# First diffusion step: where the rows of a block are scaled and split

## The chip, the cores and the metric

One core of a Trainium2 chip runs the whole kernel. The metric is the device time of one execution in microseconds (us). Five queues of instructions matter: TensorE (PE, matrix products and transposes), VectorE (DVE), ScalarE (ACT), GpSimd (POOL, which here also issues the stores) and SyncE (SP, which here issues the loads). Each of them works through its own instructions in order and waits for the others by semaphores.

## The reference

The program has two layers over 2708 nodes with 512 features. The first is graph attention with eight heads, and the change doesn't touch it. The second is a diffusion of two steps; its core, with `S` the adjacency matrix plus the unit matrix and `X` the cleared rows, is:

```python
Rf = S / S.sum(axis=1, keepdims=True)
Rb = S / S.sum(axis=0)[:, None]
Xf, Xb, Xa = X, X, X
for s in range(2):
    A = adj_from_feats(Xa, W1, W2, W3)   # logits, sorted, kept up to 0.9 of the softmax mass
    Xf = Rf @ Xf
    Xb = Rb @ Xb
    Xa = A @ Xa
    Z = Z + (Xf @ U1[s] + Xb @ U2[s] + Xa @ U3[s])
```

`A` keeps, in each row, the largest logits until their softmax reaches 0.9, and divides by their sum. In the first step `Xf` and `Xb` both start from `X`, so `S @ X` is computed once and its rows are scaled twice: by 1/row sum for `Xf` and by 1/column sum for `Xb`.

## The kernel before

The rows are cut into 22 tiles of 128 (the last has 20 rows), the tiles into 11 pairs, and two pairs make a group of four tiles (the last group has two). The second layer runs the loop `for g in range(-1, NP)` (line 1183), once for each of its two steps. One turn of the loop, called block g here, does these things for pair g and its neighbours:

- the logits of pair g + 2: `lg[g + 2].products()` (lines 511 to 524). TensorE multiplies (line 521), ScalarE copies the product from PSUM into the tile `p` (line 523). `p` has four buffers, two pairs of tiles, so these copies wait until the search of pair g has ended.
- the search for the cut of pair g + 1: `search` (line 584 on). VectorE goes over the row of logits in a few rounds (line 629), then, in `finish`, takes out the next values (lines 806 and 808) and writes the kept values into `keep` (line 730). A switch follows that is hardly ever taken (line 890) and a reciprocal (line 907). `finish` stands behind `late()`, so everything that `late` gives VectorE to do comes before it in VectorE's queue.
- the attention product of pair g: `attended` (line 1008 on), twelve steps, six for each of the two tiles. In each, TensorE transposes four 128 x 128 pieces of `keep` (line 1016), ScalarE copies them to `at` (line 1020) and TensorE multiplies them with the values (line 1035).
- the exponentials and looks of pair g + 2, which prepare its search: a list of 19 steps named `fills`, mostly ScalarE work of 2.55 us over a whole row (lines 553 and 560). The argument `first` of `attended` says from which step on they are dealt out: two at a step up to the ninth, then one, and one each at six places of `mixed`. `first` is 3, and 7 in block 0. What is left over follows at the end of the block.
- the three products with `U1`, `U2`, `U3`: `mixed` (line 1060 on), called the U phase here: twelve times a load of `u_k` and its matrix products (line 1076). Then come the keys of the next step (`project`, line 160) and the sum `yo` (lines 1089 to 1095).
- `S @ X`: `part` (line 943 on). Block g works on half of the 22 products of one group: odd blocks finish what even blocks begin. A product (line 967) is a load of 512 KB (`hl`) and one of 256 KB (`s_r`) and eight matrix products into four PSUM tiles, which are held until the group is complete. When the second half is done, each of the four tiles is scaled twice: `scaled` (line 970 on) copies it from PSUM with the factor (ScalarE, line 977, tile `xe`, four buffers), stores it to `xfb_d` (POOL, line 978) and splits it into a high and a low part by `split_rows` (VectorE, lines 181 and 182, tile `split_hl`, two buffers), which are stored to `fhl_d` or `bhl_d` (POOL, line 183). These two are read in the second step alone, `xfb_d` in the U phases of the group's own pairs, by `diffused` (line 1000).

The order on TensorE, ScalarE, VectorE and SyncE is that in which the program text issues the instructions; GpSimd's order is set by a scheduler. The text has a list `others` with the block's products and scalings, from which `paced` takes a few at each step:

```python
others = left + part(half, g + 2)
...
if not last:
    paced(others, 1 + i)
```

So in the first step (`last` is false) one is taken at each of the first six steps of `attended`, two at each of the last six, and one with each `u_k`. In an odd block the 11 products and the first scalings so fall into `attended` and the rest of the eight scalings into the U phase. The eight of block -1 are left over to block 0: four ahead of its logits and four after them.

Of the kernel before, what the change touches and what calls it, by code (L numbers as in the profile page):

```python
# [53 lines left out]
def kernel(  # L54
# [19 lines left out]
    nc = tc.nc  # L74
# [127 lines left out]
    with ExitStack() as l0:  # L202
# [13 lines left out]
        with tc.tile_pool(name="l0w", bufs=1) as wp, tc.tile_pool(name="l0p", bufs=2) as pp, \  # L216
# [44 lines left out]
            for t in range(NT):  # L261
                pr = rows[t]
# [651 lines left out]
    for s in range(STEPS):  # L914
        last = s == STEPS - 1
        with ExitStack() as st:
# [26 lines left out]
            def part(half, b):  # L943

                if b // 2 >= len(quads):
                    return []
                quad = quads[b // 2]  # L950
                first = b % 2 == 0
                w = len(quad) * P
                hl_d = (fhl_d if first else bhl_d) if last else vhl_d
                cs = range(NT) if last else range(0, NT // 2) if first else range(NT // 2, NT)
                steps = []

                def product(c):
                    if c == 0:
                        half[:] = [ps_s.tile([P, D], F32, name=f"q{i}") for i in range(len(quad))]
                    hl = sp.tile([P, 2, D], F32R, name="hl", bufs=3)  # L960
                    nc.sync.dma_start(out=hl.bitcast(F32), in_=hl_d[c * P:(c + 1) * P])
                    s_r = sp.tile([P, 2 * G * P], F32R, name="s_r")
                    nc.sync.dma_start(out=s_r[:, :w].bitcast(F32),
                                      in_=s_d[c * P:(c + 1) * P, quad[0] * P:quad[0] * P + w])
                    for j in range(len(quad)):
                        for h in range(2):
                            nc.tensor.matmul(half[j], lhsT=s_r[:, j * P:(j + 1) * P], rhs=hl[:, h],  # L967
                                             start=(c == 0 and h == 0), stop=(c == NT - 1 and h == 1))

                def scaled(t, ps, i, inv, to):  # L970
                    pr = rows[t]

                    if last and b < 2 and t % 2:
                        x = work.tile([P, D], F32, name="xw", bufs=2)
                    else:
                        x = work.tile([P, D], F32, name="xe", bufs=2 if last else 4)
                    nc.scalar.activation(x[:pr], ps[:pr], AF.Copy, scale=inv[:pr, t:t + 1])  # L977
                    nc.gpsimd.dma_start(out=xfb_d[i, cols[t], :], in_=x[:pr])
                    if not last:
                        split_rows(parts, nc.vector, x[:pr], t, to)  # L980

                steps += [lambda c=c: product(c) for c in cs]
                if last or not first:
                    for j, t in enumerate(quad):
                        if first or not last:
                            steps.append(lambda j=j, t=t: scaled(t, half[j], 0, rinv, fhl_d))
                        if not first:
                            steps.append(lambda j=j, t=t: scaled(t, half[j], 1, cinv, bhl_d))
                return steps

            def paced(steps, n):
                for step in steps[:n]:
# [12 lines left out]
            def attended(grp, keep, rden, fills, others, then, first=3):  # L1005

                def turned(i, t, cs):
                    pr = rows[t]
                    pt = ps_t.tile([P, TG, P], F32, name="t")
                    at = work.tile([P, TG, P], F32, name="at")
                    for j, c in enumerate(cs):
                        nc.tensor.transpose(pt[:rows[c], j, :pr], keep[i][:pr, cols[c]], ident[:pr, :pr])  # L1016
                    full = sum(rows[c] == P for c in cs)
                    for r, j0, j1 in ((P, 0, full), (rows[cs[-1]], full, len(cs))):
                        if j0 < j1:
                            nc.scalar.copy(at[:r, j0:j1, :pr], pt[:r, j0:j1, :pr])  # L1020
                    return at

                steps = [(i, t, cs) for i, t in enumerate(grp) for cs in tgroups]
                at = turned(*steps[0])
                xa = []
                total = len(others)
                for n, (i, t, cs) in enumerate(steps):
                    pr = rows[t]
                    nxt = turned(*steps[n + 1]) if n + 1 < len(steps) else then()
                    if n >= first:  # L1030
                        paced(fills, 1 + i if last else 1 if n > 8 else 2)
                    if cs[0] == 0:
                        pa = ps_a.tile([P, D], F32, name="a")
                    for j, c in enumerate(cs):
                        nc.tensor.matmul(pa[:pr], lhsT=at[:rows[c], j, :pr], rhs=va[:rows[c], c, :],  # L1035
                                         start=(c == 0), stop=(c == NT - 1))
                    if not last:
                        paced(others, 1 + i)
                    elif i or len(grp) == 1:
                        paced(others, (total + 10) // 13)  # L1040
                    if cs[-1] == NT - 1:
                        xa.append(work.tile([P, D], F32, name="xa"))
                        nc.scalar.activation(xa[i][:pr], pa[:pr], AF.Copy, scale=rden[:pr, i:i + 1])  # L1043
                        if not last:
                            nc.gpsimd.dma_start(out=xa_d[cols[t], :], in_=xa[i][:pr])
                    at = nxt
                    yield
                return xa, at
# [8 lines left out]
            def turned_rows(grp, v):  # L1057
                return [transposed(up, ps_t, v[i], rows[t], "v_t") for i, t in enumerate(grp)]

            def mixed(grp, v_t, xf, xb, xa, others, fills, final=False):  # L1060

# [6 lines left out]
                for n, u in enumerate((u3, u1, u2) if final else (u1, u2, u3)):  # L1070
                    nxt = turned_rows(grp, ((xf, xb) if final else (xb, xa))[n]) if n < 2 else None
                    for k in range(KD):
                        u_k = up.tile([P, D], F32, name="u_k", bufs=4 if last else 3)
                        nc.sync.dma_start(out=u_k, in_=u[s, k * P:(k + 1) * P, :])  # L1074
                        for i, t in enumerate(grp):
                            nc.tensor.matmul(pz[i][:rows[t]], lhsT=v_t[i][:, k, :rows[t]], rhs=u_k,  # L1076
                                             start=(n == 0 and k == 0), stop=(n == 2 and k == KD - 1))
                        paced(others, 1)
                        if n < 2 and k < 3:
                            paced(fills, 1)  # L1080
                    if n == 2 and not last and not final:
                        for i, t in enumerate(grp):
                            project(small, ps_t.tile([P, 512], F32, name="t"), v_t[i], t, s + 1)
                    v_t = nxt
                out_ = []
                for i, t in enumerate(grp):
                    pr = rows[t]
# [76 lines left out]
            with tc.manual_schedule(engines={PE, ACT, DVE, SP}):  # L1164
# [9 lines left out]
                half = []  # L1174
                lg += [Logits(pools, s, grp, keys, rank) for grp in pairs[1:2]]
                lg[1].queries()
                for step in part(half, 0):
                    step()
                values()
                done = []  # L1180
                ready = None
                looks, left = [], []
                for g in range(-1, NP):

                    fills = []

                    held = len(left)
                    paced(left, held if last else held // 2)
                    others = left + part(half, g + 2)
                    left = []  # L1190
                    if g == 0 and last:
                        paced(others, 4)
                    if g + 2 < NP:
                        lg[g + 2].products()
                    if g + 3 < NP:
# [4 lines left out]

                    rows_in = []
                    if g >= 0:
                        others.insert(0 if g else len(others) // 3, lambda g=g: rows_in.extend(diffused(pairs[g])))
                        final = g == NP - 1 and not last
                        att = attended(pairs[g], *ready, fills, others,
                                       lambda: None if final else turned_rows(pairs[g], rows_in[0]),
                                       3 if g else len(tgroups) + 1)
                    if g == 0:

                        paced(others, held - held // 2 if not last else 0)  # L1210
                        while looks:
                            next(att)
                            paced(looks, 2)

                    def early(g=g):
                        if g + 2 < NP:
# [3 lines left out]
                    def late(g=g):  # L1220
                        if g >= 0:
                            if g:
                                paced(others, 1)
                            xa, v_t = rest_of(att)
                            done.extend(mixed(pairs[g], v_t, *rows_in, xa, others, fills, final))
                            paced(others, len(others))
                            paced(fills, len(fills))
                            return
# [49 lines left out]
```

## Time and profile before

| | us |
|---|---|
| median of three runs | 3710.2 (3706.5 to 3715.3) |
| profiled execution | 3708.3 |
| span of its trace | 3706.5 |
| the first diffusion step in it, about | 1090 to 2300 |
| one block of it, from line 160 to line 160 | 102 to 110, in blocks 2 to 7 |

The profile has one execution. A line of a timeline names its start and length, the engine, the source line, the operation with its output and inputs, and in square brackets how long the engine had been idle before it and who ended the wait. A line of the waits names the waiting engine and instruction, the instruction that released it, the sum of such waits, their number and the longest. By stretches, from line 160 of one block to line 160 of the next, blocks 2 to 5 look like this (columns: stretch, its length, then the busy time and number of instructions of TensorE, its weight loads, VectorE, ScalarE and GpSimd, the granted clock of TensorE, the busy share of the DMA engines and what they moved):

```profile
1413.40:1520.40 107.00, 98.51 (x334) 55.59 (x333) 69.44 (x181) 60.61 (x74) 17.05 (x27) 0.95 0.41 136
1520.40:1623.70 103.30, 97.90 (x333) 54.66 (x332) 40.41 (x60) 64.22 (x82) 21.79 (x43) 0.98 0.58 201
1623.70:1730.00 106.30, 98.15 (x334) 55.16 (x333) 69.18 (x181) 60.61 (x74) 16.79 (x27) 0.97 0.41 137
1730.00:1831.90 101.90, 96.51 (x334) 53.96 (x333) 39.04 (x60) 64.22 (x82) 21.82 (x43) 1.00 0.57 204
```

All four have the same matrix products. The odd ones (second and fourth line) have the scalings besides: more ScalarE work, more stores, and less of VectorE's, because part of the search of an odd block lies beyond the cut.

### The profile page before, as it was taken

To read this page: it belongs to the slowest core of one execution; us is meant where nothing else is said; L and a number is where in the kernel's file an instruction comes from. 1 tells how busy PE (TensorE), PEld (TensorE's weight loads), DVE (VectorE), ACT (ScalarE), POOL (GpSimd) and SP (SyncE) were. 2 spreads that over 40 slices of the span, in tenths; PEclk is the share of its full clock that TensorE was granted. 3 is DMA by queue.
4 is the path that set the end of the run, shared out by engine and by line. 5 is a ranking of instruction groups with operands and counts; after the bars stand their busy time and mean duration, and the time that the engine had idled before them with its cause. 6 is when DMAs were issued, how large, how long until landed. Compare 5 with 4: busy or idle time off the path is not lost. (4 is left out here: it accounts for less than half of the span.)

```text
span 3706.5 us, 35338 instructions
## 1 busy us (share of the span) xinstructions
PE 3367.4 (91%) x11143; PEld 1754.4 (47%) x11143; DVE 2612.9 (70%) x4820; ACT 1541.5 (42%) x2334; POOL 799.6 (22%) x1119
## 2 busy tenths in 40 slices
PE   7998999998966988989899899688999999999898
PEld 4433333333444545545455453445655565556452
DVE  4588888889957637365463651969988779777991
ACT  2343212111114674655666612345654556445511
POOL 4114140514331112121202121302112111121101
PEclk9999999999978999999999999999999999999999
DMA  3477424233228445454535353966556665566552
GB/s 113 152 252 243 137 80 150 80 105 103 74 87 278 164 157 187 145 183 149 205 131 196 128 191 100 302 203 225 175 187 208 233 216 204 183 213 234 201 201 66
DMA packets 276459, 634.08 MB, mean 171 GB/s; under 512 B 37210, under 2 KB 70442, under 8 KB 273244
## 3 DMA queue, kind: packets, MB, share of 16 engines
q1 hardware_dynamic: 249183, 540.99, 44.2%
q0 software_dynamic: 27024, 90.30, 6.3%
q8 instruction: 89, 1.46, 0.2%
q14 instruction: 163, 1.33, 0.1%
HBM read 509.07 MB, written 122.10 MB: 170 GB/s over the span
## 5 line engine op out<-in xcount | busy, mean ns | idle before, releaser
L1035 PE MATMUL a<-va,at 128*128 128x512 f32 (+2 forms) x1936 | 890.1, 599 | 14.0 <-ACT at L1020 13.5
L967 PE MATMUL q<-hl,s_r 128*128 128x512 f32 x2904 | 820.9, 429 | 62.5 <-DMA s_r<-s_d 62.2
L429 PE MATMUL po<-e,fw 128*65 128x512 f32 (+4 forms) x2112 | 838.7, 552 | 34.3 <-DVE e L427 21.8
L427 DVE SCALAR_TENSOR_TENSOR e<-r_b,kk,a_c 128x512 f32<-128x512 f32 (+4 forms) x1056 | 751.8, 741 | 73.5 <-PE po L429 23.7
L967 PEld LDWEIGHTS q<-hl,s_r 128*128 128x128 f32 x2904 | 544.4, 190 | 307.5 <-issue 133.2
L553 ACT ACTIVATE junk_a<-p,nth 128x2708 uint8<-128x2708 f32 (+1 forms) x240 | 613.1, 2554 | 70.6 <-POOL nth L572 66.8
L429 PEld LDWEIGHTS po<-e,fw 128*65 128x65 f32 (+1 forms) x2112 | 286.2, 140 | 546.7 <-issue 269.2
L1035 PEld LDWEIGHTS a<-va,at 128*128 128x128 f32 (+2 forms) x1936 | 337.1, 187 | 379.4 <-issue 342.7
L1076 PE MATMUL a<-u_k,v_t 128*128 128x512 f32 (+1 forms) x1056 | 489.9, 601 | 22.3 <-ACT xa L1043 15.4
L629 DVE SCALAR_TENSOR_TENSOR junk<-p,th 128x2708 bf16<-128x2708 f32 (+1 forms) x132 | 401.2, 3039 | 4.0
L1020 ACT COPY at<-t 128x512 f32<-128x512 f32 (+3 forms) x308 | 140.4, 477 | 494.5 <-PE t L1016 494.1
L1076 PEld LDWEIGHTS a<-u_k,v_t 128*128 128x128 f32 (+1 forms) x1056 | 188.9, 187 | 242.1 <-issue 182.9
L521 PE MATMUL t<-keys,q_t 128*128 128x452 f32 x528 | 167.1, 443 | 118.4 <-ACT p L523 98.1
L181 DVE TENSOR_SCALAR split_hl<-xe 128x512 int32<-128x512 int32 (+1 forms) x44 | 19.1, 434 | 257.1 <-ACT xe L977 210.7
L808 DVE MAX8 vn<-keep 128x8 f32<-128x2708 f32 (+1 forms) x66 | 196.8, 2981 | 2.3
L523 ACT COPY p<-t 128x452 f32<-128x452 f32 (+2 forms) x264 | 132.0, 538 | 126.5 <-PE t L521 82.3
L521 PEld LDWEIGHTS t<-keys,q_t 128*128 128x128 f32 x528 | 91.7, 211 | 189.2 <-ACT p L523 150.7
L411 ACT ACTIVATE s_c<-a_c 128x512 fp32r<-128x512 f32 (+3 forms) x132 | 76.1, 577 | 247.5 <-DMA a_c<-in_adj_t_dram 120.7
L1016 PE MATMUL t<-ident,keep 128*128 128x128 f32 (+1 forms) x968 | 147.2, 274 | 27.1 <-DVE keep L757 19.2
L1016 PEld LDWEIGHTS t<-ident,keep 128*128 128x128 f32 (+1 forms) x968 | 115.0, 139 | 107.5 <-issue 79.5
L548 DVE TENSOR_REDUCE nmx<-p 128x1 f32<-128x2708 f32 (+1 forms) x44 | 129.0, 2966 | 41.7 <-ACT p L523 41.7
L565 POOL TENSOR_TENSOR x<-sums,powers 128x4 f32<-128x4 f32 x22 | 44.7, 2033 | 508.7 <-ACT p L560 508.7
(296 smaller groups left out, 3151.9 us busy)
## 6 DMA issues: line engine op xcount, KB each, us to landing
s_r<-s_d SPq DMA_DIRECT2D x330, 256.0 KB
hl<-vhl_d SPq DMA_DIRECT2D x132, 512.0 KB
u_k<-in_L_gnn_U_dram SPq DMA_DIRECT2D x264, 256.0 KB
hl<-fhl_d SPq DMA_DIRECT2D x132, 512.0 KB
hl<-bhl_d SPq DMA_DIRECT2D x132, 512.0 KB
arow<-in_adj_dram SPq DMA_DIRECT2D x21, 1354.0 KB
s_d<-s_c SPq DMA_DIRECT2D x88, 256.0 KB
a_c<-in_adj_t_dram SPq DMA_DIRECT2D x84, 256.0 KB
```

Source lines behind the costliest of these rows:

```text
L427: nc.vector.scalar_tensor_tensor(e[:pr, :cw], r_b[:pr, i, :cw], kk[:pr, t, hd:hd + 1], a_c[t][:pr, :cw], op0=OP.max, op1=OP.mult)
L429: nc.tensor.matmul(po[i][:, :cw], lhsT=fw[:pr, t, hd, :], rhs=e[:pr, :cw], start=(t == 0), stop=(t == NT - 1))
L521: nc.tensor.matmul(pl[:, :c1 - c0], lhsT=q[:, i], rhs=self.keys[:, c0:c1], start=(i == 0), stop=(i == 1))
L523: nc.scalar.copy(p[:pr, c0:c1], pl[:pr, :c1 - c0])
L553: nc.scalar.activation(junk[:pr], self.p[i][:pr], func, **kw)
L629: v.scalar_tensor_tensor(junk_b[:pr], ps_[i][:pr], th, ps_[i][:pr], op0=OP.is_ge, op1=OP.mult, accum_out=dst)
L808: v.max(vs, keep[0][:pr])
L967: nc.tensor.matmul(half[j], lhsT=s_r[:, j * P:(j + 1) * P], rhs=hl[:, h], start=(c == 0 and h == 0), stop=(c == NT - 1 and h == 1))
L1016: nc.tensor.transpose(pt[:rows[c], j, :pr], keep[i][:pr, cols[c]], ident[:pr, :pr])
L1020: nc.scalar.copy(at[:r, j0:j1, :pr], pt[:r, j0:j1, :pr])
L1035: nc.tensor.matmul(pa[:pr], lhsT=at[:rows[c], j, :pr], rhs=va[:rows[c], c, :], start=(c == 0), stop=(c == NT - 1))
L1076: nc.tensor.matmul(pz[i][:rows[t]], lhsT=v_t[i][:, k, :rows[t]], rhs=u_k, start=(n == 0 and k == 0), stop=(n == 2 and k == KD - 1))
```

## The change

`part` returns two lists now, the products and the scalings. `scaled` no longer splits at once: it scales and stores, and returns a function that splits. In the first step the scalings of an odd block are kept out of `others`. Half of them are issued at the end of the U phase by `half_scaled`, between the keys and the copies of `yo`; their splits are kept in `held` and issued at the start of the next block, behind the whole search. The other half, with its splits, comes in the next block behind its logits. Block 0 is done as before.

The dealing changes with it. In `attended` one item of `others` is taken in two of three steps (not at steps 0, 3, 6 and 9) and never two, so that eight of the twelve (eleven products and the loads of `diffused`) fall there, one ahead of it, and three into the U phase. In even blocks that had scalings left over, `diffused` comes after two products instead of first, and `first` is 5 instead of 3. In the second step the lists are joined again, and what is left of `others` after the U phase is issued before the copies of `yo` instead of after them.

```diff
@@ part @@
                 if b // 2 >= len(quads):
-                    return []
+                    return [], []
...
                     nc.gpsimd.dma_start(out=xfb_d[i, cols[t], :], in_=x[:pr])
-                    if not last:
-                        split_rows(parts, nc.vector, x[:pr], t, to)
+                    return lambda: None if last else split_rows(parts, nc.vector, x[:pr], t, to)
 
                 steps += [lambda c=c: product(c) for c in cs]
+                scales = []
                 if last or not first:
                     for j, t in enumerate(quad):
                         if first or not last:
-                            steps.append(lambda j=j, t=t: scaled(t, half[j], 0, rinv, fhl_d))
+                            scales.append(lambda j=j, t=t: scaled(t, half[j], 0, rinv, fhl_d))
                         if not first:
-                            steps.append(lambda j=j, t=t: scaled(t, half[j], 1, cinv, bhl_d))
-                return steps
+                            scales.append(lambda j=j, t=t: scaled(t, half[j], 1, cinv, bhl_d))
+                return steps, scales
@@ attended @@
                     if not last:
-                        paced(others, 1 + i)
+                        paced(others, 1 if n % 3 else 0)
@@ mixed @@
-            def mixed(grp, v_t, xf, xb, xa, others, fills, final=False):
+            def mixed(grp, v_t, xf, xb, xa, others, fills, final, also):
...
                     v_t = nxt
+                also()
                 out_ = []
@@ the loop @@
-                for step in part(half, 0):
-                    step()
+                for steps in part(half, 0):
+                    paced(steps, len(steps))
...
-                looks, left = [], []
+                looks, left, held = [], [], []
+
+                def split(rows_):
+                    for row in rows_:
+                        row()
+                    del rows_[:]
+
+                def scaled_and_split(scales_, n):
+                    for step in scales_[:n]:
+                        step()()
+                    del scales_[:n]
+
                 for g in range(-1, NP):
...
-                    held = len(left)
-                    paced(left, held if last else held // 2)
-                    others = left + part(half, g + 2)
-                    left = []
+                    if g == 0:
+                        scaled_and_split(left, len(left) if last else len(left) // 2)
+                    others, scales = part(half, g + 2)
                     if g == 0 and last:
                         paced(others, 4)
+                    if last:
+                        others += scales
+                        scales = []
+
+                    split(held)
                     if g + 2 < NP:
                         lg[g + 2].products()
...
-                        others.insert(0 if g else len(others) // 3, lambda g=g: rows_in.extend(diffused(pairs[g])))
+                        others.insert(len(others) // 3 if g == 0 else 2 if left else 0, lambda g=g: rows_in.extend(diffused(pairs[g])))
...
-                                       3 if g else len(tgroups) + 1)
+                                       len(tgroups) + 1 if g == 0 else 5 if left else 3)
                     if g == 0:
 
-                        paced(others, held - held // 2 if not last else 0)
+                        scaled_and_split(left, len(left))
                         while looks:
                             next(att)
                             paced(looks, 2)
+                    else:
+                        scaled_and_split(left, len(left))
+                    left = scales
+
+                    def half_scaled():
+
+                        paced(others, len(others))
+                        if g > 0:
+                            for step in left[:len(left) // 2]:
+                                held.append(step())
+                            del left[:len(left) // 2]
...
-                            done.extend(mixed(pairs[g], v_t, *rows_in, xa, others, fills, final))
+                            done.extend(mixed(pairs[g], v_t, *rows_in, xa, others, fills, final, half_scaled))
```

## The prediction

> **What bounds the kernel now.** I read the page's engine table first, then who waited for whom over the first diffusion step (1180 to 2230 us, all that the change touches), then TensorE's timeline there, and last the queues behind its gaps.
>
> ```profile
> PE 3367.4 (91%) x11143; PEld 1754.4 (47%) x11143; DVE 2612.9 (70%) x4820; ACT 1541.5 (42%) x2334; POOL 799.6 (22%) x1119
> DVE split_hl L181 <- ACT xe L977: 210.7, 10, 42.8
> ```
>
> TensorE (PE) is busy 91% of the span, so time is to be won only in its gaps. VectorE (DVE) lost 210.7 us in ten waits for scaled rows; that matters only where it makes PE late. The timeline of PE shows where. L160 is the last work of a block, L521 the logits at the start of the next, L1035 its first attention product.
>
> ```profile
> 1498.59 7.35 PE L1076 MATMUL a<-u_k,v_t 128*128 128x512 f32 x16
> 1520.38 1.95 PE L160 MATMUL t<-v_t,kw 128*128 128x128 f32 x16
> 1524.27 1.12 PE L521 MATMUL t<-keys,q_t 128*128 128x452 f32 x4 [0.74 <-ACT p L523]
> 1600.01 7.97 PE L1076 MATMUL a<-u_k,v_t 128*128 128x512 f32 x14 [2.33 <-ACT xa L1043]
> 1609.88 14.00 PE L1076 MATMUL a<-u_k,v_t 128*128 128x512 f32 x32 [1.02 <-DMA u_k<-in_L_gnn_U_dram]
> 1623.71 1.95 PE L160 MATMUL t<-v_t,kw 128*128 128x128 f32 x16
> 1634.79 7.52 PE L521 MATMUL t<-keys,q_t 128*128 128x452 f32 x20 [7.92 <-ACT p L523]
> ```
>
> Block 2 (even, ends 1520) scales no rows: its U phase (L1076) has no gap and the next logits wait 0.74 us. Block 3 (odd, ends 1624) scales eight: gaps of 2.33 and 1.02 us in U, then 7.92 us. VectorE's timeline tells why:
>
> ```profile
> 1586.65 0.43 DVE L181 TENSOR_SCALAR split_hl<-xe 128x512 int32<-128x512 int32 x1 [42.79 <-ACT xe L977]
> 1606.72 3.03 DVE L806 SCALAR_TENSOR_TENSOR keep<-p,th 128x2708 f32<-128x2708 f32 x1
> 1638.02 0.17 DVE L907 RECIPROCAL rden<-den 128x2 f32<-128x2 f32 x1 [5.18 <-issue]
> ```
>
> It stands 42.79 us before the first split; the end of the search (L806 on) starts only when all splits are done, 1606.72, and ends with L907 at 1638, and the logits' copies into `p` wait for it.
>
> **What the Trainium skill says.** "Perfetto Trace Analysis", Sequencer Loop: an engine instruction waits in its engine's queue until its semaphores are ready; the 42.79 us with the search behind it agree. "DMA: Bandwidth & Descriptors", Issuing engines are not separate DMA queues: transfers issued by SP and POOL interleave on the same 16 DMA engines; this fits the `u_k` waits, seen in odd blocks, where the rows' stores are out, and not in blocks 2, 4 and 6. "SBUF — State Buffer", Who interferes with whom: a VectorE instruction with two SBUF inputs and a GpSimd one that reads SBUF exclude each other; the L565 power on POOL took 3.72 us at 1463.46, beside VectorE's L806 of 1463.24, and 1.04 us at 1351.83.
>
> **Part 1, the search is no longer behind the splits (blocks 1, 3, 5, 7).** In the built order four splits stand after L907 and four more after that. Then the search waits, as in block 2, for the last transposes of `keep` (second L730 at 1491.55, some 15 us before L160 with its branch), so the 8.20, 7.92, 10.95 and 6.37 us gaps go. What is late next is a queue that the change itself makes. I count from the start of L160 to the first L1035: 20.67, 19.93, 23.18 and 18.24 us in the profile, sum 82.0; from block 2 to 3 it is 11.75.
>
> New at this joint: ScalarE (ACT) has its two keys done at 2.4 (from 1520.38), then four scalings at 0.57 apart (4.7), two `yo` copies (5.7), the logits' copies, which end 2.3 later than in block 2, at 13.1, then four more scalings, then the first `at` copy. The `xe` tile has four buffers and `split_hl` two: scaling 7 needs split 3, and split 3 needs the landing of the first `fhl_d` store, which POOL issues behind its key work, two `yo` additions, their stores, and now four `xfb_d` stores:
>
> ```profile
> 1522.00 0.46 POOL L170 TENSOR_TENSOR kq_hl<-kq_b,kq_hl 128x128 f32<-128x128 f32 x1 [12.68 <-ACT kq_b L166]
> 1530.09 0.57 POOL L1095 DMA_DIRECT2D y_d<-yo  x1 [0.30 <-POOL yo L1093]
> ```
>
> That queue ends at 10.3 after L160; four stores of 0.54 make it 12.5. From there the profile has the very chain, once, at the start of block 0:
>
> ```profile
> 1201.18 0.54 POOL L183 DMA_DIRECT2D fhl_d<-split_hl  x1 [11.71 <-DVE split_hl L182]
> 1205.43 0.69 ACT L977 ACTIVATE xe<-q,rinv 128x512 f32<-128x512 f32 x1 [1.84 <-issue]
> 1206.85 0.69 ACT L977 ACTIVATE xe<-q,cinv 128x512 f32<-128x512 f32 x1 [0.73 <-DVE split_hl L182]
> 1207.44 1.06 ACT L1020 COPY at<-t 128x512 f32<-128x512 f32 x2
> ```
>
> Store issued 1201.18, last scaling done 1207.54: 6.4 us. So scaling 8 ends at 12.5 + 6.4 = 18.9. PE has meanwhile moved one product (2.1 us) ahead of the transposes and its last two matmuls need the eighth row out of PSUM: 0.5, transposes 0.4, copy 0.6, wakeup 0.1: the first L1035 at 20.5. The product is only moved, so 18.4 is to be compared, three times; in block 8 the new group has two tiles, whose buffers are free, so 19.7 less 1.05 = 18.65. Sum 73.9: gain 8.1 us. Bounds for scaling 8: 15.4 if POOL were no limit (13.1 + 2.3), gain 14 more; about 24 if POOL is slowed and the landing is the slowest, loss 20. I take 18.9, the measured chain.
>
> **Part 2, the U phase of odd blocks.** First L1076 to L160: 26.42, 27.06, 25.59 and 28.01 us in blocks 1, 3, 5, 7 (sum 107.1), 21.79 in 2, 4 and 6. The excess is ScalarE's scalings ahead of `xa` (2.33 each) and `u_k` arriving late beside eight 256 KB and eight 512 KB stores. Both leave: 107.1 - 87.2 = 19.9 us gain. In exchange three products (768 KB of loads each) come into every U phase. Nearest row: the second diffusion step interleaves a product with each `u_k`, 2783 to 2820 us, without a wait for a load; so I charge nothing. Lower bound: only the 9.3 us of `xa` goes and 10.6 us of load waits stay.
>
> **Part 3, the looks start later in even blocks (5 instead of 3).** Of 19 steps, 2 x 4 + 3 + 6 = 17 are placed before the end of the U phase, against all 19 now. One look (2.55 + 0.19 us on ScalarE) falls behind `yo`, before the logits' copies: 2.7 us of PE gap after blocks 2, 4, 6 and, ahead of the `at` copy, 8. Loss 10.8 us. The later start is cover: VectorE's eight splits end at about 27 after L160 (four splits took 7 us at 1199.7 to 1206.8), then 3.9 to the first mass, 7.1 to the maximum, 3.0 for it: 41. ScalarE reaches it at the sixth attention step, 20.5 + 23.4 = 44. Three microseconds of margin; each one beyond costs PE about as much.
>
> **Part 4, products in two of three attention steps.** The same eleven products are issued. A bare step is 3.9 us of PE against 6.1 of ScalarE (copy and two looks), one with product 5.8. Adding both queues up from the third step, ScalarE is 0.3 us late once in an odd block and never in a full even one: 1.2 us. Block 8, with half products, loses 0.63 + 1.77 + 1.08 us already and stays there: nothing. Block 0 keeps its 13.95 us gap, as its start of looks is unchanged.
>
> **Part 5, the last joint (block 9 to 10).** Four scalings, 2.3 us, stand before the first `at` copy, and no logits cover them. Loss 2.3 us. SP's queue: the `xfb_d` loads stand behind two products in blocks 2, 4, 6, 8, and POOL issues the stores that these wait for ahead of the `yo` additions; nothing. In the second step two scalings change place with two `yo` copies on ScalarE: nothing.
>
> **Sum.** 8.1 + 19.9 - 10.8 - 1.2 - 2.3 = 13.7 us less. The profiled execution took 3708.3 us (span 3706.5), so 3694.6; the median of the runs is 1.9 higher, 3710.2, hence 3696.5.
>
> **Rivals.**
> A, the joint is not bound by POOL: scaling 8 at 15.4 instead of 18.9, four times 3.5: 14 us more gain, 3682. For it: the landing in part 1 was the quick kind (3.0 us, median 3.4). Against: the built order has the store behind four others and two additions. Chance 0.10.
> B, the `u_k` waits stay, now behind the products' loads: 10.6 us back, 3707, no change to be measured. For it: this step has three buffers for `s_r` and `u_k`, the second four. Against: only three of twelve `u_k` meet a product. Chance 0.20.
> C, slower: the store chain at the start of blocks 2, 4, 6, 8. Every microsecond of it is one on ScalarE's queue before the first `at` copy, and on PE four times over. It cancels the gain at 3.4 us more per block and shows as slower at 5.3. Landings of these stores reached 6.4 us, and a POOL operation beside VectorE's wide ones took 2.30 us instead of 0.46 (1415.01); 6 us each give 24 - 13.7 = 10 more, 3720. Against: VectorE is idle or in the short splits then. Chance 0.17.
> That the change doesn't reach its aim, the search still ending late, I give no share: the order has no split before L907 in these blocks.
>
> **How the numbers follow.** Forecast 0.53; alone it spans 3689 to 3704 (1 us of joint is 4, U phase stalls up to 0.5 us per block). A measurement here can tell 0.2%, 7.4 us. Faster: A, and 0.50 of the forecast, 0.60; same: most of B and the forecast's tail, 0.22; slower: C and a corner of B with late maxima, 0.18. The range reaches from the forecast's low end, less a part of A, to a mild C: 3686 to 3716.
>
> **What would show it.** Right: the waits of L181 for `xe` fall from 210.7 to under 60 us and none stands before L806; odd U phases last as long as even ones plus three products; L160 to L1035 near 20.5 in even blocks and near 14.5 in odd ones. Wrong: that joint above 24 with ScalarE waiting for splits, `u_k` gaps in most blocks, or ScalarE waiting for the maximum in even blocks.

## The result and the profile after

| | us |
|---|---|
| before, median of four runs | 3711.0 (3706.5 to 3715.3) |
| changed, median of four runs | 3754.3 (3744.1 to 3763.8) |
| ratio, 95% interval | 1.0118 (1.0102 to 1.0134) |
| profiled execution of the changed kernel, and its span | 3763.8, 3762.0 |

The change costs 43 us where 13.7 less were forecast. Lines from about 948 on are one higher in the changed kernel (L977 is L978, L1035 is L1036, L1076 is L1077). The page and the waits of the first step (1180 to 2300 us), against the lines shown of before:

```profile
PE 3402.7 (90%) x11143; PEld 1771.5 (47%) x11143; DVE 2602.4 (69%) x4820; ACT 1543.9 (41%) x2334; POOL 813.1 (22%) x1119
...
DVE split_hl L181 <- ACT xe L978: 141.0, 5, 29.9
```

VectorE still stands 141 us in front of splits, where the prediction had wanted under 60, but now behind the search (each of the five waits comes after L907, the last instruction of a search, and before the next L806), where it has nothing else to do. By stretches, blocks 2 to 5 of the changed kernel (columns as in the table of before):

```profile
1413.60:1531.60 118.00, 102.78 (x333) 57.40 (x332) 59.51 (x139) 62.80 (x80) 25.46 (x40) 0.91 0.52 176
1531.60:1636.40 104.80, 98.69 (x334) 55.81 (x333) 48.33 (x101) 62.65 (x76) 15.35 (x30) 0.97 0.42 139
1636.40:1748.50 112.10, 99.69 (x333) 56.23 (x332) 59.57 (x139) 62.80 (x80) 22.80 (x40) 0.94 0.55 185
1748.50:1853.00 104.50, 97.69 (x334) 55.01 (x333) 48.34 (x101) 62.54 (x76) 15.78 (x30) 0.98 0.42 139
```

All four are longer, the even ones (first and third line) by 11.0 and 5.8 us. To see where, I cut each block in TensorE's timeline at L160, the first attention product and the first U product. "Joint" is L160 to the first attention product; the joint of block 2 is the one at its start. In the changed kernel the even joints contain a product that stood in the attention phase before (2.1 us, half of it in block 8), so the prediction is put here as it gave these joints with it, 20.5 us three times and 19.7, and the phases without it. The sums over blocks 1 to 9:

| us | before | changed | difference | predicted |
|---|---|---|---|---|
| joints of blocks 2, 4, 6, 8 | 82.0 | 100.9 | +18.9 | -0.8 |
| joints of blocks 3, 5, 7 | 35.2 | 46.1 | +10.9 | +8.1 |
| joints of blocks 1 and 9 | 30.2 | 32.7 | +2.5 | +2.7 |
| attention and U phases | 780.7 | 790.6 | +9.8 | -26.0 |
| sum | 928.1 | 970.3 | +42.2 | -16.0 |

The prediction's other 2.3 us belong to the joint of block 10, which lies behind these blocks. The even joints are 19.7 us off and the phases 35.8.

The same nine blocks as one stretch, in the kernel before and then in the changed one (columns as above):

```profile
1296.24:2224.40 928.16, 852.33 (x2877) 473.51 (x2876) 488.06 (x1064) 526.81 (x666) 174.85 (x311) 0.97 0.49 167
```

```profile
1299.87:2270.20 970.33, 873.06 (x2878) 485.47 (x2877) 474.14 (x1063) 527.76 (x662) 170.05 (x301) 0.94 0.47 157
```

Of the 42.2 us, 21.4 are more idle time of TensorE (75.8 before, 97.3 after) and 20.7 are the same matrix products taking longer, at a granted clock of 0.94 instead of 0.97. So about half of the loss isn't waiting but slow matrix products, which follow waits of TensorE (the last section shows them).

The other 13 us of this profile's excess lie outside these blocks. Of these, 3.6 are there before block 1 begins, 7.6 come between the start of block 10 and the first logits of the second step, and 2.0 after the last logits of that step; between these logits both kernels take 1100.5 us. So the second step neither gained nor lost. Two of the four runs are 18 to 20 us shorter than this one.

The end of block 2 and of block 3, then the even joint that follows, in TensorE's timeline:

```profile
1517.90 13.90 PE L1077 MATMUL a<-u_k,v_t 128*128 128x512 f32 x32
1531.64 1.95 PE L160 MATMUL t<-v_t,kw 128*128 128x128 f32 x16
...
1622.62 13.90 PE L1077 MATMUL a<-u_k,v_t 128*128 128x512 f32 x32
1636.36 1.95 PE L160 MATMUL t<-v_t,kw 128*128 128x128 f32 x16
1638.06 1.45 PE L521 MATMUL t<-keys,q_t 128*128 128x452 f32 x4
1642.55 4.62 PE L521 MATMUL t<-keys,q_t 128*128 128x452 f32 x12 [3.04 <-ACT p L523]
```

The U phase of odd block 3 ends like that of even block 2, without a gap (27.03 us each), and the 7.92 us wait of the logits behind block 3 is a 3.04 us one, for ScalarE's four scalings and two `yo` copies. So far the change does what was predicted. The loss comes right after, here in the joint of block 2, in the timelines of all engines:

```profile
1425.59 0.67 POOL L183 DMA_DIRECT2D fhl_d<-split_hl  x1
1427.13 1.09 PE L968 MATMUL q<-hl,s_r 128*128 128x512 f32 x4
1432.01 0.43 DVE L181 TENSOR_SCALAR split_hl<-xe 128x512 int32<-128x512 int32 x1 [12.57 <-DMA fhl_d<-split_hl]
1433.24 0.69 ACT L978 ACTIVATE xe<-q,rinv 128x512 f32<-128x512 f32 x1 [4.21 <-issue]
1436.18 0.69 ACT L978 ACTIVATE xe<-q,cinv 128x512 f32<-128x512 f32 x1 [2.25 <-DVE split_hl L182]
1436.92 1.22 PE L968 MATMUL q<-hl,s_r 128*128 128x512 f32 x2 [7.10 <-ACT xe L978]
1439.67 2.90 PE L1036 MATMUL a<-va,at 128*128 128x512 f32 x4
```

POOL issues the first `fhl_d` store 11.96 us after L160. The third split starts 6.42 us later, when that store has landed; the last two scalings follow it, and TensorE's product waits 7.10 us for the eighth row to leave PSUM. In these 6.4 us the DMA engines are busy at 1.00 (0.59 in the three microseconds of the same landing in block 0 of the kernel before), and not with stores alone: SP issues the four `xfb_d` loads from 1421.22 on and the loads of a product at 1426.37 and 1426.92. A second loss lies in the attention phase of the same block:

```profile
1475.67 3.04 DVE L806 SCALAR_TENSOR_TENSOR keep<-p,th 128x2708 f32<-128x2708 f32 x1
1476.43 3.17 POOL L565 TENSOR_TENSOR x<-sums,powers 128x4 f32<-128x4 f32 x1 [5.18 <-ACT p L560]
1481.91 3.03 DVE L806 SCALAR_TENSOR_TENSOR keep<-p,th 128x2708 f32<-128x2708 f32 x1
1482.01 3.04 POOL L572 TENSOR_SCALAR nth<-th_a 128x6 f32<-128x6 f32 x1
1485.08 2.55 ACT L553 ACTIVATE junk_a<-p,nth 128x2708 uint8<-128x2708 f32 x1 [6.77 <-POOL nth L572]
1490.93 6.29 PE L1036 MATMUL a<-va,at 128*128 128x512 f32 x8 [3.87 <-ACT at L1021]
```

POOL computes the points `nth` between L565 and L572, small operations on a few numbers. L565 takes 1.04 us and L572 0.26 where they don't meet VectorE's wide pass L806; here both meet it and end just behind it (0.9 and 0.1 us), the points come 5 us later, ScalarE waits 6.77 us for them, two looks then stand ahead of its `at` copy, and TensorE waits 3.87 us. Over the step, ScalarE's waits for the points, before and then after the change (the sum, their number and the longest):

```profile
ACT junk_a L553 <- POOL nth L572: 11.6, 4, 5.0
```

```profile
ACT junk_a L553 <- POOL nth L572: 45.9, 9, 8.4
```

Before, L565 took 3.72 us in blocks 2, 4 and 6 and 1.04 in the others, and these attention phases lasted 64.5 us like those of blocks 1, 3, 5 and 7: such points cost TensorE nothing, as the late steps had two products each.

### The profile page after: what moved, and what is told of

Read it like the earlier page. It is cut to its first block, busy times and chain, and to the rows that moved or that the text cites. A ratio compares the mean times of both kernels' runs of the same rounds, so it can differ in the third digit from the quotient of the medians.

```text
span 3762.0 us, 35377 instructions
## 1 busy us (share of the span) xinstructions
PE 3402.7 (90%) x11143; PEld 1771.5 (47%) x11143; DVE 2602.4 (69%) x4820; ACT 1543.9 (41%) x2334; POOL 813.1 (22%) x1119
## 5 line engine op out<-in xcount | busy, mean ns | idle before, releaser
L1036 PE MATMUL a<-va,at 128*128 128x512 f32 (+2 forms) x1936 | 908.2, 609 | 45.9 <-ACT at L1021 45.9
L968 PE MATMUL q<-hl,s_r 128*128 128x512 f32 x2904 | 834.3, 432 | 87.5 <-DMA s_r<-s_d 63.7
L427 DVE SCALAR_TENSOR_TENSOR e<-r_b,kk,a_c 128x512 f32<-128x512 f32 (+4 forms) x1056 | 751.0, 740 | 77.6 <-PE po L429 28.6
L1036 PEld LDWEIGHTS a<-va,at 128*128 128x128 f32 (+2 forms) x1936 | 343.6, 190 | 424.1 <-issue 354.3
L1077 PE MATMUL a<-u_k,v_t 128*128 128x512 f32 (+1 forms) x1056 | 489.6, 598 | 7.2 <-ACT xa L1044 5.2
L1077 PEld LDWEIGHTS a<-u_k,v_t 128*128 128x128 f32 (+1 forms) x1056 | 189.0, 186 | 209.8 <-issue 176.2
L1017 PE MATMUL t<-ident,keep 128*128 128x128 f32 (+1 forms) x968 | 149.8, 278 | 26.2 <-DVE keep L757 19.2
L149 ACT COPY v_t<-t 128x512 f32<-128x512 f32 (+1 forms) x132 | 68.6, 571 | 177.1 <-PE t L147 177.1
```

The source lines that it names most:

```text
L427: nc.vector.scalar_tensor_tensor(e[:pr, :cw], r_b[:pr, i, :cw], kk[:pr, t, hd:hd + 1], a_c[t][:pr, :cw], op0=OP.max, op1=OP.mult)
```

## The experiments

The times of before were 3709.2 us in the set of experiments 1 to 4, 3709.3 in that of 5 to 8 and 3711.8 in that of 9 and 10; the ratios are to these. The changed kernel's 3754 us come from its own set (before 3711.0), so a difference to it is good to a few microseconds, and its runs lie in two pairs, near 3745 and near 3763.

**1. The old pacing alone put back.**

```diff
-                        paced(others, 1 if n % 3 else 0)
+                        paced(others, 1 + i)
```

> The changed kernel with the old pacing of the products alone put back: one in the first attention step, two in the second and so on, instead of one in two steps of three. Theory (the thin steps uncover ScalarE's lateness, which two products in a step used to cover): the attention phases of blocks 1 to 8 lose most of their stalls (36 us in the changed kernel, counted as phase minus 44.3 minus 1.84 per product), 25 to 35 us back, about 3720 to 3728. Rival (the pacing is harmless, the time went to the joints of the even blocks): attention phases as in the changed kernel, about 3754. Either way the joints of blocks 2, 4 and 6 stay near 25 to 26 us.

Measured: 3723.9 us, ratio 1.0042 (1.0028 to 1.0056), 30 us off the changed kernel. The odd attention phases last 64.5 us with eleven products, exactly as before the change; joints of blocks 2, 4, 6: 25.8, 25.3, 25.3. The thin steps cost about 30 us, and the joints are another matter.

**2. The sums behind the held splits.**

```diff
-                for i, t in enumerate(grp):
-                    y = work.tile([P, D], F32, name="yo")
...
-                        nc.gpsimd.dma_start(out=y_d[cols[t], :], in_=y[:pr])
+                pending.append(evacuated)      # the same lines, as a function
...
                     split(held)
+                    split(pending)
```

> The changed kernel with the copies of yo, POOL's additions and the y_d stores of a block issued after the held splits at the start of the next block. Theory (the fhl_d store is late because it stands behind the additions and y_d stores in POOL's queue): it is issued about 3 us earlier and the joints of blocks 2, 4, 6 and 8 fall from 25.2 to about 20 to 22 us, 14 to 25 us in sum, about 3730 to 3740. Rival (the landing takes its 6.4 us because of the traffic of the DMA engines, whoever stands ahead in the queue; and ScalarE still has the yo copies to do before the at copy): joints within 2 us of the changed kernel, about 3750.

Measured: 3730.8 us, 1.0061 (1.0042 to 1.0079), 23.5 us off. The joints of blocks 2, 4, 6 and 8 are 19.4, 19.0, 19.0 and 17.7. Its timeline at the joint of block 2, where L160 started at 1408.53:

```profile
1416.95 0.68 POOL L183 DMA_DIRECT2D fhl_d<-split_hl  x1
1421.81 0.43 DVE L181 TENSOR_SCALAR split_hl<-xe 128x512 int32<-128x512 int32 x1 [7.45 <-DMA fhl_d<-split_hl]
```

The store is issued 8.42 us after L160, 3.5 earlier, and lands in 4.86 us instead of 6.42. So its place in POOL's queue counts, and the landing is shorter besides. What makes the landing long isn't separated: here six stores were issued in the seven microseconds ahead of it instead of seven, and no loads of a product beside it.

**3. The points first.** VectorE's wide pass is made to wait for POOL's points by a small copy ahead of it; pacing and joints stay as in the changed kernel.

```diff
                             xa, v_t = rest_of(att)
+                            if not last and g + 2 < NP:
+                                seen = small.tile([P, NA, G], F32, name="seen", bufs=1)
+                                nc.vector.tensor_copy(seen, lg[g + 2].nth)
```

> The changed kernel with one small VectorE copy of the points that POOL computes for the search of the next block but one, placed before the end of the search, so that VectorE's wide two-input pass starts only when POOL has them. Theory (the two exclude each other, and the points come late because VectorE is now in that pass at that time): the power L565 and the points L572 fall from about 3 us each to about 1 and 0.3 us, ScalarE's wait for nth from 45.9 us to under 15, and 10 to 20 us of TensorE's stalls in the attention phases go: about 3735 to 3745. Rival (POOL is slow for reasons of its own, or ScalarE is late without it): L565 and L572 as before, no change, about 3754.

Measured: 3723.9 us, 1.0039 (1.0025 to 1.0053): 30 us off the changed kernel, more than was expected and as much as experiment 1. A wait and two instructions of its profile, with the thin steps still there:

```profile
ACT junk_a L553 <- POOL nth L572: 14.1, 8, 2.9
```

```profile
1470.51 1.04 POOL L565 TENSOR_TENSOR x<-sums,powers 128x4 f32<-128x4 f32 x1 [5.18 <-ACT p L560]
1473.95 0.26 POOL L572 TENSOR_SCALAR nth<-th_a 128x6 f32<-128x6 f32 x1
```

The odd attention phases are 59.6 us, against 59.0 for eight products without a stall (64.5 less three products of 1.84; with and without one, the transposes of two steps are 5.71 and 3.87 us apart in its timeline). Thin steps cost next to nothing when the points come early: the loss needs both.

**4. The aim alone, on the kernel before:** splits behind the search, but from the rows that `diffused` loads back, so that no scaling waits for the store of a split and nothing moves on TensorE.

```diff
-                    if not last:
-                        split_rows(parts, nc.vector, x[:pr], t, to)
...
+                    if g >= 0 and not last:
+                        for xs, to in zip(rows_in, (fhl_d, bhl_d)):
+                            for t, x in zip(pairs[g], xs):
+                                split_rows(parts, nc.vector, x[:rows[t]], t, to)
```

> The kernel before with one edit: the rows are split not from the scaled tile but from the tile that is loaded back for the diffusion, after the search of the block, four rows in every block; nothing is moved on TensorE. It has the aim of the change (no split stands ahead of the search) without the wait of a scaling for a store and without thin steps. Theory (the stall before was VectorE's queue alone): the joints of blocks 2, 4, 6 and 8 (20.7, 19.9, 23.2, 18.2 us) fall to about 12, 25 to 35 us in sum, while the waits of 2.33 us for xa stay in the odd blocks: about 3675 to 3685. Rival (VectorE's stall was cover for POOL's points, which now meet the end of the search as in the changed kernel): the attention phases give back 10 to 25 us, about 3690 to 3705.

Measured: 3684.2 us, 0.9929 (0.9912 to 0.9945). The joints of blocks 2, 4, 6 and 8 are all 11.7 us, 35 us less in sum. L565 now takes 3.3 us in the mean of nine, so POOL is held up in most blocks, and yet the attention phases of blocks 1 to 7 are 64.5 us: with double products the late points cost nothing. The U phases lose 15 us, waiting for `u_k` beside the stores of the splits.

**5. Both edits, 1 and 2, on the changed kernel.**

> The changed kernel with both edits together: the old pacing of the products, and the yo copies, additions and y_d stores behind the held splits. Theory (the two losses are separate: one in the attention phases, one in the joints of the even blocks): the gains add, 30 and 23.5 us off 3754, so 3700 (3695 to 3706), which leaves of the change what its other parts were priced at. Rival (they hide one another, the joint's time coming back in the attention phase or the other way round): 3712 to 3722.

Measured: 3702.7 us (twelve runs), 0.9985 (0.9976 to 0.9993). The gains add: 51.5 us off the changed kernel, against 30.4 and 23.5 alone. What is left stands 6 us from the forecast of 3696.5. That is in part chance: the even joints sum to 74.8 us, better than the 81.2 that were forecast, as the sums now stand behind them, and in return ScalarE waits for the first maximum:

```profile
ACT nmx L556 <- DVE nmx L548: 15.9, 4, 6.0
```

**6. The thin steps alone, on the kernel before, in even blocks.**

```diff
-                        paced(others, 1 + i)
+                        paced(others, 1 + i if total > 11 else 1 if n % 3 else 0)
```

> The kernel before with the new pacing alone, and only in blocks 2, 4, 6 and 8: one product in two steps of three, so eight in the attention phase and three in the U phase. Nothing else is moved. Theory (thin steps alone uncover the late points of POOL, which in these blocks already met VectorE's wide pass before the change): these attention phases take 3 to 7 us more than 59.0 us (44.3 and eight products of 1.84; half products in block 8), 12 to 25 us in sum, about 3722 to 3735. Rival (it needs the later start of the looks and the later splits, as the prediction priced the pacing by itself): no change, 3708 to 3713.

Measured: 3720.6 us (3711.4 to 3729.7), 1.0029 (1.0019 to 1.0040): 11 us, just under what was expected and above the rival's range; the attention phases of blocks 2, 4 and 6 are 61.9, 62.1 and 62.2 instead of 59.0. In block 2 the pass meets another of POOL's operations, L573, which takes 0.23 us where it doesn't meet it:

```profile
1467.92 3.03 DVE L806 SCALAR_TENSOR_TENSOR keep<-p,th 128x2708 f32<-128x2708 f32 x1
1468.50 2.54 POOL L573 TENSOR_SCALAR thr<-sums 128x2 f32<-128x2 f32 x1
1473.42 2.55 ACT L553 ACTIVATE junk_a<-p,nth 128x2708 uint8<-128x2708 f32 x1 [3.65 <-POOL nth L572]
1490.66 3.70 PE L1035 MATMUL a<-va,at 128*128 128x512 f32 x8 [1.75 <-ACT at L1020]
```

The pacing alone is worth a measurable loss. In the changed kernel it is 30: the odd blocks, where VectorE no longer stands still, have it too (1.4 to 3.6 us above 59.0 in each of blocks 1, 3, 5 and 7), and in even blocks more of POOL's operations meet the pass (in blocks 6 and 8 both L565 and L572, as in block 2).

**7. Experiment 4 with four scalings of odd blocks held until the attention phase is over.**

```diff
-                        paced(others, 1 + i)
+                        paced(others, min(1 + i, max(0, len(others) - (4 if total > 14 else 0))))
```

> The kernel before with the splits taken from the loaded rows after the search, and besides the last four scalings of odd blocks held until after the attention phase, so that ScalarE has four fewer ahead of xa. Theory (xa waits for the scalings ahead of it): the four waits of 2.33 us at the start of the odd U phases go, 5 to 9 us less than with the splits moved alone, about 3675 to 3679. Rival (the four scalings then stand ahead of the copies of the turned rows, and the wait only moves by some microseconds): within 3 us of 3684.

Measured: 3674.8 us, 0.9912 (0.9895 to 0.9928), 9.4 us less than experiment 4, the upper end of what was expected. The wait for `xa` in block 3 is 0.62 us instead of 2.33, and the U phases of blocks 3, 5 and 7 last 25.2, 25.2 and 26.2 us instead of 27.8 to 28.7. That of block 1 stays at 28.6, as it waits for `u_k`.

**8. Experiment 5 with the looks of even blocks from step 3 on.**

```diff
-                                       len(tgroups) + 1 if g == 0 else 5 if left else 3)
+                                       len(tgroups) + 1 if g == 0 else 3)
```

> The changed kernel with both edits (old pacing, sums later) and the looks of even blocks started in step 3 again instead of 5. The prediction priced the later start at 2.7 us in each of four joints. If that holds, and the cover is not needed: 8 to 11 us less than with the two edits alone, about 3690. If VectorE's splits make the first maximum late, as the trace of the changed kernel has it (maximum 46 to 52 us after L160 where the looks of the fifth step want it at 44): ScalarE waits 5 to 8 us for it in each even block ahead of its at copies, no gain or up to 20 us more, 3700 to 3720.

Measured: 3738.7 us, 1.0083 (1.0066 to 1.0100), 36 us more than experiment 5 and well above both ranges: of the two it is the second, at twice its price. The attention phases of blocks 2, 4 and 6 take 76 us. In block 2:

```profile
1462.43 0.20 ACT L556 ACTIVATE nmx<-nmx 128x1 f32<-128x1 f32 x1 [14.63 <-DVE nmx L548]
1468.19 4.07 PE L1036 MATMUL a<-va,at 128*128 128x512 f32 x4 [9.83 <-ACT at L1021]
```

ScalarE reaches the first maximum 14.63 us too early, and its `at` copies stand behind it. The later start isn't a price that the change pays for nothing; its late splits need it. The odd joints fell to 11.7 us all the same (15.2 to 15.9 in experiment 5), so the later start does cost the odd joints what the prediction charged for it, 3.4 to 4.2 us rather than 2.7.

**9. Edits 1 and 3 together.**

> The changed kernel with two of the edits that each took 30 us off by themselves: the old pacing, and VectorE's wide pass held until POOL has the points. Theory (both end the same loss: late points that thin steps don't cover): together no more than either alone, 3718 to 3727. Rival (two losses that happen to be of one size): 3690 to 3700.

Measured: 3726.2 us, 1.0037 (1.0023 to 1.0052). Nothing is added: early points and thick steps end the same loss.

**10. Experiment 7 with three `xe` buffers for four and four `u_k` buffers for three.**

> The kernel with the splits moved to the loaded rows and four scalings held, with one xe buffer fewer (three) and one u_k buffer more (four). Theory (what is left in its U phases, 1.9 to 4.8 us above 21.8, is u_k loads late beside the stores, and a deeper queue of loads covers it): 5 to 15 us less than 3674.8, 3660 to 3670. Rival (the loads are late by throughput, not by depth, or three xe buffers make the scalings wait for their stores ahead of the at copies): 3670 to 3685.

Measured: 3653.5 us, 0.9844 (0.9828 to 0.9860), better than expected. TensorE's group of U products in experiment 7, then here (busy, mean of one in ns, idle ahead of it and who ended it; L1074 and L1041 are L1076 and L1043 of the kernel before):

```profile
L1074 PE MATMUL a<-u_k,v_t 128*128 128x512 f32 (+1 forms) x1056 | 496.1, 604 | 29.8 <-DMA u_k<-in_L_gnn_U_dram 20.8 <-ACT xa L1041 8.7
```

```profile
L1074 PE MATMUL a<-u_k,v_t 128*128 128x512 f32 (+1 forms) x1056 | 486.9, 597 | 9.3 <-ACT xa L1041 8.6 <-DMA u_k<-in_L_gnn_U_dram 0.3
```

The waits for `u_k` are gone, so the loads were late by depth, that is by how few of them could be under way, and not by throughput. Blocks 1 to 9 take 876.4 us instead of 928.1. Two of them, by stretches:

```profile
1410.20:1508.40 98.20, 96.10 (x334) 54.11 (x333) 56.87 (x123) 59.95 (x74) 21.65 (x31) 1.00 0.52 176
1508.40:1607.30 98.90, 96.19 (x334) 53.92 (x332) 53.40 (x121) 64.12 (x82) 23.82 (x39) 1.00 0.53 185
```

## Why the prediction was wrong

- **Part 1, the even joints: the step failed.** The issue of the store was right (11.96 us after L160, 12.5 predicted). Wrong was what followed: "Store issued 1201.18, last scaling done 1207.54: 6.4 us", taken from block 0. It was 1425.59 to 1436.87, 11.3 us. In block 0 POOL had issued no store in the 11.7 us before it; here it had issued seven in the seven microseconds before, and SP's loads were under way too. Part 5 had put these loads at nothing. I had the place of it, rival C with landings of 6.4 us, and gave it 0.17. The term is 19.7 us off (joints of 26.0, 25.3, 25.7 and 23.9 us against 20.5 three times and 19.7), part of it the slower clock after the wait, which I had not priced at all. The Trainium skill ("DMA: Bandwidth & Descriptors", Anatomy of one DMA — SWDGE (gpsimd) path) gives 2.0 us and the bytes at 436 GB/s, an estimate of 3.2 us for 512 KB; the quick landing in block 0 (3.0) agrees, the landings in the busy joints (6.42, and 4.86 in experiment 2) do not, and the measured ones are what a buffer waits for.
- **Part 2, the U phases: right.** Odd U phases have no wait for `xa` and none for `u_k` of note, the products' loads cost nothing (27.03 us is 21.79 and three products of 1.75 each), and rival B fell. The two parts that failed hide this gain in the total.
- **Part 3, the looks: near in price, wrong in the margin, by luck without harm.** Its cost showed in the odd joints (+10.9 against +8.1) and in that of block 9 (6.42 us, 2.5 more, against 2.7). The first maximum was ready 47.6 to 50.0 us after L160 in blocks 2, 4, 6 and 8, not 41. ScalarE waited for it only once, for 1.6 us, because the late joint had made ScalarE late as well; with the joint shorter in experiment 5 it waits four times. Experiment 8 shows what happens without the later start.
- **Part 4, the thin steps: the step failed.** "ScalarE is 0.3 us late once in an odd block and never in a full even one" added up ScalarE's and TensorE's queues and left POOL's points out, as if they came in time. In the odd blocks of the trace of before they did, because VectorE stood waiting for scaled rows, and in blocks 2, 4 and 6, where L565 took 3.72 us, the two products of a step hid it. The change takes both covers away. The prediction quoted the Trainium skill for just this exclusion ("SBUF — State Buffer", Who interferes with whom) and L565 with its 3.72 us, and did not carry it into the sum of this part. Priced 1.2 us; about 30 measured (experiments 1 and 3). Block 8, where nothing was priced, is hit too: L565 and L572 take 3.82 and 3.04 us there, and TensorE waits 5.98.
- **Part 5, the last joint (block 9 to 10): right** (6.20 us instead of 3.98, so 2.2 more against 2.3).
- **The aim** was right: experiment 4 reached it without the two losses, and experiment 5 shows that without most of them the change stands 6 us from the forecast, in part by chance, as said there.

What stays open: whether stores or loads make the landing long, what the 13 us of the profile outside blocks 1 to 9 come from in detail, and why the changed kernel's runs lie 20 us apart. Experiment 6, with thin steps only, spreads over 18 us, and experiment 3, with thin steps and early points, over 7, so chance meetings of POOL and VectorE are likely; it wasn't tested by itself.

## What to carry to other kernels

A stall that a change removes may be the cover of something else: before taking it away, look for short operations on other engines that run in it, and price them as they run beside the engine when it is busy. Work that is dealt out evenly between the steps of a loop gives less cover than the same work dealt in double portions where the slow partner is late. A store's landing measured in a quiet stretch is no price for the same store in a busy one; where a buffer waits for a landing, take the slowest landing in the trace, or take the buffer from a tile that is loaded anyway; and a TensorE wait of more than about two microseconds is to be priced with the slow matmuls that may follow it.

## What the runs showed of the hardware

- A GpSimd operation of 0.2 to 1 us that started within VectorE's wide pass L806 ended 0.1 to 0.9 us after the end of that pass: L565 took 3.17 us instead of 1.04, L573 2.54 instead of 0.23, L572 3.04 instead of 0.26. It hit any one of the chain, in some blocks two. With the pass held back until POOL was done (experiment 3) all nine of each took their short time.
- A wait of TensorE cost more than its length. After the 3.87 us wait of block 2 eight matmuls took 6.29 us instead of 3.60, and shorter waits were followed by slow ones too, here one of block 6 of the changed kernel and one of experiment 2:

```profile
1929.71 5.36 PE L1036 MATMUL a<-va,at 128*128 128x512 f32 x8 [3.00 <-ACT at L1021]
```

```profile
2071.48 5.35 PE L1036 MATMUL a<-va,at 128*128 128x512 f32 x8 [2.26 <-ACT at L1021]
```

- The slow stretch can begin a microsecond late. After the 3.04 us wait of the logits at 1642.55 the granted clock is 0.50 from 1643.5 to 1645.5 us, and after the wait of 2.33 us in block 3 of the kernel before it is 0.50 from 1601 to 1604, while the same wait in block 1 (1390.33) left it at 1.00. Waits of some 1.74 us in blocks 3, 5 and 7 of the changed kernel had eight matmuls of 3.70 us behind them, but one of 1.68 us at 2335 was followed by a clock of 0.50. The Trainium skill ("TensorE: Matmul & The Clock Gate", Part 1: The HAM clock gate) says that the clock is halved after an idle window of about 3.4 us; the half clock agrees, the length doesn't, as waits of 2.3 to 3.3 us were enough here, most of the time.
- Over blocks 1 to 9 the slow matmuls are 20.7 us of the 42.2. In experiment 10, with one long wait left in these blocks (13.95 us, at the start of block 1), the same products are busy for 840.7 us instead of 852.3 before, more than a fifth of the 51.8 us that it gains there.
